# A decoder layer with a routed MoE on one core: expert weights kept for two phases, tanh in the router, wider steps in the norms

## The chip, the cores and the metric

The kernel runs on one core of one Trainium2 chip. The metric is device time in microseconds (us) of one execution. A core has TensorE (PE, with its weight loads shown apart as PEld), VectorE (DVE), ScalarE (ACT), GpSimd (POOL) and SyncE (SP), each with an instruction queue of its own that is worked off in order, and 16 DMA engines that they share.

## What is computed

A transformer decoder layer in float32 on `x` and a context, both (32, 128, 128): 32 sequences of 128 tokens with 128 features. 16 heads of 8 features, 8 experts with 512 hidden features, two experts per token.

```python
def _attn(q_in, k_in, v_in, wq, bq, wk, bk, wv, bv, wo, bo, causal):
    ...
    scores = jnp.einsum('bqhd,bkhd->bhqk', Q, Kp) / jnp.sqrt(jnp.float32(HD))
    if causal:
        mask = jnp.tril(jnp.ones((Sq, Sk), bool))
        scores = jnp.where(mask, scores, -jnp.inf)
    a = jax.nn.softmax(scores, axis=-1)
    o = jnp.einsum('bhqk,bkhd->bqhd', a, V).reshape(Bq, Sq, Dm)
    return o @ wo + bo

def _moe(x, rw, rb, w1, b1, w2, b2):
    ...
    router_weights = jax.nn.softmax(xf @ rw + rb, axis=-1)
    topw, topi = jax.lax.top_k(router_weights, K)
    topw = jax.nn.softmax(topw, axis=-1)
    combine = jnp.zeros((T, E), xf.dtype).at[jnp.arange(T)[:, None], topi].add(topw)
    h = jax.nn.gelu(jnp.einsum('td,edf->etf', xf, w1) + b1[:, None, :], approximate=False)
    eo = jnp.einsum('etf,efd->etd', h, w2) + b2[:, None, :]
    out = jnp.einsum('etd,te->td', eo, combine)
    return out.reshape(x.shape)

x = _layernorm(x + _attn(x, x, x, ..., True), ln1_g, ln1_b)
x = _layernorm(x + _attn(x, encoder_output, encoder_output, ..., False), ln2_g, ln2_b)
x = _layernorm(x + _moe(x, router_w, router_b, e_w1, e_b1, e_w2, e_b2), ln3_g, ln3_b)
```

## The kernel before, in words

**Attention.** Sequences go in groups of four. A unit is one sequence of self- (`s`) or cross-attention (`c`); 64 units run in a hand-written order, two half slots each. A half slot makes PE score one unit twice: `sc`, from which DVE takes the row maxima (L465), and two units later `st`, transposed and with the maxima subtracted, which ACT exponentiates (L473) and, for causal units, POOL masks (L477). Values, outputs and the splitting of the maxima (POOL, L491 to L494) follow in later half slots.

**Chores.** All else of a group (turning and projecting inputs, layer norm, routing, placing tokens, the biases) is written as generators. Each `yield` ends a step; `chain` and `book` put each step into a half slot by hand-written costs (`NORM`, `ROUTE`, `PLACE`: one tuple of PE, DVE, ACT and POOL times for a step) inside a window of half slots. The order of instructions on every queue is the order in which the program issues them; nothing is moved afterwards.

**Layer norm** (`normalize`): DVE statistics (L330) | DVE aggregates (L333), POOL adds epsilon and raises to −0.5 (L334, L335) | DVE makes the shift (L337) | ACT scales and shifts two sequences (L340) | ACT the other two. A bar is a `yield`. It runs 16 times in attention and 8 times on the outputs (`finish`).

**Routing** (`route`): PE logits, DVE adds the bias and subtracts the maximum (L617 to L620) | ACT exponential (L622) | DVE softmax and the eight largest (L625 to L631) | DVE their places (L634) and the difference of the two largest | ACT tanh (L640), which makes the softmax of two. `place` then counts each token's row in a table ordered by expert.

**Blocks.** Tokens' rows are scattered by POOL into a buffer in HBM (`xs`, L762, 64 scatters, one per half slot at the earliest), in two phases of four groups. Each phase has 39 blocks of 128 rows: blocks 0 to 7 belong to experts 0 to 7 and are called fixed; the expert of the other 31 is read from a table in memory (L830). A block fetches its expert's weights on SP (`wd`, 514 KB, L827 fixed or L831 dynamic), four blocks ahead into five buffers. Four blocks share a fetch of rows (`xt`, L814) and a turn: four transposes on PE (L843), four small DVE steps and the copy to `xT` (L858). A block is first layer (`ph`, PE, L866), Gelu with bias (ACT, four instructions, L871), second layer (`po`, PE, L882, one block later), copy to `ot` (DVE, L887, four buffers) and scatter to `eo` (POOL, L889).

**Beside the blocks.** `run` calls `beside` after each block. While half slots are left (the end of attention, the last routings, the row scatters of the second phase) it runs one per block; then it steps up to two `combine` generators. `combine` fetches the base (`x2d`, L955) and gathers a group's results (`gt`, L957), adds them with their weights (DVE, L974), and `finish` normalizes and applies gain and bias (L983, L985) and writes (L987).

**The start of the blocks**: at half slot `start − 6` the first four weights are fetched (`prepare`), at `start − 1` the first rows (`first_rows`), and `run` begins with the first turn.

Of the kernel before, what the change touches and what calls it, by code (L numbers as in the profile page):

```python
# [17 lines left out]
P = 128  # L18
# [44 lines left out]
def kernel(  # L63
# [260 lines left out]
    def normalize(y, name):  # L324
# [11 lines left out]
        yield  # L336
        nc.vector.scalar_tensor_tensor(rs[:, 1], mv[:, :, 0], -1.0, rs[:, 0], ALU.mult, ALU.mult)  # L337
        yield
        for t in range(G):
            nc.scalar.activation(  # L340
                y[:, t, :], y[:, t, :], AF.Identity,
                bias=rs[:, 1, t : t + 1], scale=rs[:, 0, t : t + 1],
            )
            if t == 1:
                yield
# [240 lines left out]
    def biases(gr):  # L586
# [8 lines left out]
        yield  # L595
        pw = mm_tile([G * E, P], f"pw_{gi}")
        nc.tensor.transpose(pw, w[:, 0].rearrange("p b e -> p (b e)"), ident)
        wT = small.tile([G * E, P], F32, tag="wT", name=f"wT_{gi}", bufs=2)
        nc.scalar.copy(wT, pw)
# [8 lines left out]
    def route(gr):  # L608
# [12 lines left out]
        yield  # L621
        nc.scalar.activation(lg, lg, AF.Exp)  # L622
        yield
        ls = small.tile([P, G], F32, tag="ls", name=f"ls_{gi}")
        nc.vector.tensor_reduce(ls, lg, AX.X, ALU.add)  # L625
        nc.vector.reciprocal(ls, ls)
        nc.vector.tensor_tensor(lg, lg, bc(ls, 2, E), ALU.mult)
# [4 lines left out]
        yield  # L632
        for b in range(G):
            nc.vector.max_index(idx[:, b, :], top[:, b, :], lg[:, b, :])  # L634


        ex = small.tile([P, G], F32, tag="ex", name=f"ex_{gi}")
        nc.vector.tensor_tensor(ex, top[:, :, 0], top[:, :, 1], ALU.subtract)
        yield
        nc.scalar.activation(ex, ex, AF.Tanh, scale=0.5)  # L640
# [11 lines left out]
        nc.vector.tensor_scalar(wts[:, 0, bs], ex, 0.5, 0.5, ALU.mult, ALU.add)  # L652
        nc.vector.tensor_scalar(wts[:, 1, bs], ex, -0.5, 0.5, ALU.mult, ALU.add)
# [124 lines left out]
    def pack_biases():  # L778
# [3 lines left out]
        nc.vector.tensor_copy(b1T, pb)  # L782
        nc.sync.dma_start(
# [11 lines left out]
    def weights(name):  # L795
        return moe.tile([P, 1, WP], F32, tag="wd", name=f"wd_{name}", bufs=AHEAD + 1)

    class Blocks:
# [23 lines left out]
        def fetch_weights(self, i):  # L822
            if i >= self.n:
                return
            wd = weights(f"{self.ph.p}_{i}")
            if i < NS:
                nc.sync.dma_start(out=wd[:, 0, :], in_=wpk[i])  # L827
            else:
                d = i - NS
                e = nc.sync.value_load(self.ph.tab[0:1, d : d + 1], min_val=0, max_val=E - 1)  # L830
                nc.sync.dma_start(  # L831
                    out=wd, in_=wpk[bass.ds(e, 1), :, :].rearrange("e p w -> p e w")
                )
            self.w[i] = wd[:, 0, :]
# [25 lines left out]
        def first_layer(self, i):  # L860
            w, name = self.w[i], f"{self.ph.p}_{i}"
# [8 lines left out]
            for c in range(NFC):  # L870
                nc.scalar.activation(  # L871
                    self.h[i][:, c, :], hid[:, c, :], AF.Gelu, bias=w[:, B1 + c : B1 + c + 1]
                )

        def second_layer(self, i):
# [3 lines left out]
            w, h = self.w.pop(i), self.h.pop(i)  # L879
            po = mm_tile([P, P], f"po_{p}_{i}")  # L880
            for c in range(NFC):
                nc.tensor.matmul(  # L882
                    po, lhsT=h[:, c, :], rhs=w[:, W2 + c * P : W2 + (c + 1) * P],
# [16 lines left out]
    class Pipeline:  # L900


        def __init__(self, *blocks):
            self.all = [(k, i) for k in blocks for i in range(k.n)]
            self.quads = [(k, q) for k in blocks for q in range(-(-k.n // XB))]
            self.turned = 0

        def weights(self, j):
            if j < len(self.all):
                k, i = self.all[j]  # L910
                k.fetch_weights(i)

        def prepare(self):
            for j in range(AHEAD):
                self.weights(j)
# [14 lines left out]
        def run(self, beside):  # L930

            self.turn()
            before = None
            for j, (k, i) in enumerate(self.all):
                self.weights(j + AHEAD)
# [45 lines left out]
    def finish(gr):  # L981
        yield from normalize(gr.acc, f"m{gr.gi}")
# [82 lines left out]
    NORM = (dve(1.2), (0.0, 0.9, 0.0, 1.3), dve(0.2), dve(0.0, 0.7), dve(0.0, 0.7))  # L1065
    TURN = (pe(0.45, 0.4),) * 2
    PROJECT = (pe(0.45, 0.0, 0.4),) * 2
    ROUTE = (pe(0.3, 0.0, 0.9), dve(0.0, 0.2), dve(1.2), dve(1.1), dve(0.8), dve(0.4))
# [3 lines left out]
    for gi in range(NG):  # L1072
# [36 lines left out]
        ends = chain(ends[10], ends[10] + 5, (lambda c=c: route(c), *ROUTE))  # L1109
# [149 lines left out]
```

## Time and profile before

| | |
|---|---|
| median of 9 runs | 654.76 us (650.47 to 660.95) |
| the profiled execution | 659.73 us |
| its span in the profile | 658.0 us |
| PE busy | 569.4 us, 87% of the span |
| PEld busy | 477.8 us, 73% |
| DVE busy | 409.9 us, 62% |
| ACT busy | 404.5 us, 61% |
| POOL busy | 366.9 us, 56% |
| DMA packets | 82.48 MB, mean 125 GB/s |
| attention's half slots | 0 to about 448 us, 128 of them |
| first and last block's first layer | 451.22 and 634.54 us |
| last instruction | about 658 us |

The profile follows one execution. A line of the timeline gives start, duration, engine, line of the program, operation, `out<-in` by the program's names, shapes, and how many instructions it joins; in brackets the idle time of the engine ahead of it and whose work ended that. `<-issue` is idle time in which the engine waited for nothing that the profile shows. In the list of waits a line gives engine, tile and line, what it waited for, the sum in us, how many times, and the longest. Durations are read from single instructions or means of a group; a group that joins instructions has their sum as it runs.

### The profile page before, as it was taken

To read this page: it belongs to the slowest core of one execution; us is meant where nothing else is said; L and a number is where in the kernel's file an instruction comes from. 1 tells how busy PE (TensorE), PEld (TensorE's weight loads), DVE (VectorE), ACT (ScalarE), POOL (GpSimd) and SP (SyncE) were. 2 spreads that over 40 slices of the span, in tenths; PEclk is the share of its full clock that TensorE was granted. 3 is DMA by queue.
4 is the path that set the end of the run, shared out by engine and by line. 5 is a ranking of instruction groups with operands and counts; after the bars stand their busy time and mean duration, and the time that the engine had idled before them with its cause. 6 is when DMAs were issued, how large, how long until landed. Compare 5 with 4: busy or idle time off the path is not lost. (4 is left out here: it accounts for less than half of the span.)

```text
span 658.0 us, 21902 instructions
## 1 busy us (share of the span) xinstructions
PE 569.4 (87%) x8812; PEld 477.8 (73%) x8863; DVE 409.9 (62%) x1321; ACT 404.5 (61%) x919; POOL 366.9 (56%) x747
## 2 busy tenths in 40 slices
PE   8798888899999798999999988988898878999870
PEld 6566667777777677777777767777888768998870
DVE  2455456465657866787688668885866635543463
ACT  4356576587577467766758677555675445675652
POOL 2365454344545456728836624644788885655561
PEclk9999899899999899999999989998999979999995
DMA  6110910923010011001001100331788989999972
GB/s 134 30 36 2 139 24 19 224 86 118 2 34 3 1 35 51 2 2 54 16 18 31 39 2 7 108 138 53 259 282 284 334 295 375 367 362 387 348 235 76
DMA packets 48038, 82.48 MB, mean 125 GB/s; under 512 B 7968, under 2 KB 26464, under 8 KB 47936
## 3 DMA queue, kind: packets, MB, share of 16 engines
q1 hardware_dynamic: 42816, 71.57, 34.4%
q0 software_dynamic: 4544, 9.38, 3.9%
q8 instruction: 69, 1.13, 0.7%
q14 instruction: 33, 0.27, 0.1%
q10 hardware_dynamic: 576, 0.13, 0.1%
HBM read 62.15 MB, written 23.10 MB: 130 GB/s over the span
## 5 line engine op out<-in xcount | busy, mean ns | idle before, releaser
L465 DVE TENSOR_REDUCE m_s<-sc_s 128x8 f32<-128x1024 f32 x64 | 78.3, 1224 | 79.6 <-PE st_s L450 63.8
L871 ACT ACTIVATE h<-ph,wd 128x128 f32<-128x128 f32 x312 | 88.6, 368 | 60.6 <-ACT h L871 20.6
L477 POOL TENSOR_SCALAR_AFFINE_SELECT pr_s<-pr_s 128x1024 f32<-128x1024 f32 x64 | 69.9, 1092 | 97.2 <-ACT pr_s L473 97.1
L889 POOL DMA_INDIRECT eo<-ot,to x78 | 77.5, 993 | 51.9 <-DVE acc L974 12.5
L473 ACT ACTIVATE pr_s<-st_s 128x1024 f32<-128x1024 f32 x64 | 65.7, 1026 | 61.3 <-PE st_s L450 59.4
L473 ACT ACTIVATE pr_c<-st_c 128x1024 f32<-128x1024 f32 x64 | 65.8, 1028 | 59.2 <-PE st_c L450 58.0
L465 DVE TENSOR_REDUCE m_c<-sc_c 128x8 f32<-128x1024 f32 x64 | 78.1, 1220 | 32.8 <-PE st_c L450 21.7
L866 PE MATMUL ph<-xT,wd 128*128 128x128 f32 x624 | 85.9, 282 | 9.9 <-DMA wd<-wpk 6.3
L882 PE MATMUL po<-wd,h 128*128 128x128 f32 x624 | 84.0, 278 | 6.0 <-ACT h L871 6.0
L866 PEld LDWEIGHTS ph<-xT,wd 128*128 128x128 f32 x624 | 77.5, 195 | 14.5 <-issue 3.8
L882 PEld LDWEIGHTS po<-wd,h 128*128 128x128 f32 x624 | 77.0, 194 | 6.6 <-ACT h L871 6.6
L457 PE MATMUL sc_c<-k_c,qb_c 32*128 32x128 f32 x1024 | 75.2, 285 | 4.6 <-DVE m_c L465 4.3
L457 PE MATMUL sc_s<-k_s,qb_s 32*128 32x128 f32 x1024 | 76.8, 289 | 0.3
L762 POOL DMA_INDIRECT xs<-x,slots x64 | 64.5, 1007 | 12.8 <-issue 12.2
L450 PE MATMUL st_c<-qb_c,k_c 32*128 32x128 f32 x1024 | 70.7, 274 | 0.0
L450 PEld LDWEIGHTS st_s<-qb_s,k_s 32*128 32x128 f32 x1024 | 70.2, 193 | 0.1
L450 PE MATMUL st_s<-qb_s,k_s 32*128 32x128 f32 x1024 | 70.1, 276 | 0.0
L450 PEld LDWEIGHTS st_c<-qb_c,k_c 32*128 32x128 f32 x1024 | 69.6, 189 | 0.5
L457 PEld LDWEIGHTS sc_c<-k_c,qb_c 32*128 32x128 f32 x1024 | 62.9, 188 | 6.3 <-DVE m_c L465 6.1
L457 PEld LDWEIGHTS sc_s<-k_s,qb_s 32*128 32x128 f32 x1024 | 64.3, 191 | 1.7 <-issue 1.7
L887 DVE COPY ot<-po 128x128 f32<-128x128 f32 x78 | 22.5, 289 | 61.9 <-PE po L882 52.6
L442 PEld LDWEIGHTS <-ones 32*128 32x128 bf16 x256 | 14.0, 91 | 46.3 <-issue 43.0
(243 smaller groups left out, 1196.9 us busy)
## 6 DMA issues: line engine op xcount, KB each, us to landing
wd<-wpk SPq DMA_DIRECT2D x78, 514.0 KB, 5.5
xs<-blank SPq DMA_DIRECT2D x2, 2600.0 KB
xt<-xs SPq DMA_DIRECT2D x20, 260.0 KB, 5.7
wpk<-in_L_xattn_e_w_dram SPq DMA_DIRECT2D x16, 256.0 KB, 10.8
gt<-eo SPq DMA_DIRECT2D x8, 512.0 KB, 6.7
xg<-in_x_dram SPq DMA_DIRECT2D x8, 256.0 KB, 3.9
eg<-in_ctx_dram SPq DMA_DIRECT2D x8, 256.0 KB
x2d<-base SPq DMA_DIRECT2D x8, 256.0 KB
```

The lines of the kernel that those rows point to most:

```text
L442: nc.tensor.matmul(st[:, i], lhsT=ones16[rowsof(g), :], rhs=old.mq[rowsof(g)], start=True, stop=False,)
L450: nc.tensor.matmul(st[:, i, r, :], lhsT=old.group.k[rowsof(g), old.b, :], rhs=old.group.qb[rowsof(g), old.b, r, :], start=False, stop=r == 3,)
L457: nc.tensor.matmul(sc[:, i, r, :], lhsT=new.group.qb[rowsof(g), new.b, r, :], rhs=new.group.k[rowsof(g), new.b, :], start=not new.masked, ...
L465: nc.vector.tensor_reduce(new.m[:, 8 * half : 8 * half + 8], sc.rearrange("p i r k -> p (i r) k"), AX.X, ALU.max,)
L473: nc.scalar.activation(old.pr[:, hs, :], st.rearrange("p i r k -> p (i r) k"), AF.Exp, scale=SCALE)
L477: nc.gpsimd.affine_select(out=old.pr[:, hs, :], in_=old.pr[:, hs, :], pattern=[[0, 8], [1, P]], compare_op=ALU.is_ge, fill=0.0, base=0, ch ...
L762: i = nc.gpsimd.indirect_dma_start(out=xs[ph.p][:, :], out_offset=bass.IndirectOffsetOnAxis(ap=slots[:, k, t : t + 1], axis=0), in_=gr.x2[ ...
L866: nc.tensor.matmul(hid[:, c, :], lhsT=w[:, c * P : (c + 1) * P], rhs=self.xT[i // XB][:, i % XB, :], start=True, stop=True,)
L871: nc.scalar.activation(self.h[i][:, c, :], hid[:, c, :], AF.Gelu, bias=w[:, B1 + c : B1 + c + 1])
L882: nc.tensor.matmul(po, lhsT=h[:, c, :], rhs=w[:, W2 + c * P : W2 + (c + 1) * P], start=c == 0, stop=c == NFC - 1,)
L887: nc.vector.tensor_copy(ot, po)
L889: s = nc.gpsimd.indirect_dma_start(out=eo[p][:, :], out_offset=bass.IndirectOffsetOnAxis(ap=self.to[q][:, i % XB : i % XB + 1], axis=0), i ...
```

## The change

**Weights.** The eight fixed experts' weights are fetched once, when phase 0 needs them, as two DMAs of 256 KB each (`w1`, `w2`), into buffers of attention that are done by then (`kvT`, `xT0`, `k`, and the two `pr`), and phase 1 uses them again. Their biases come from a tile that is already on chip. Dynamic blocks fetch as before, but by a count of dynamic blocks ahead, and one step later in SP's order. The first rows are fetched at `start − 5`, the first turn runs at `start − 2`; weights follow at `start − 6` (experts 0 to 2), `start − 1` (3 to 6) and `start + 1` (7).

**Routing.** Instead of exp(a) of the logits less their maximum it computes (1 + t) / (1 − t) with t = tanh(a / 2); the eight largest are taken before that, their places beside it.

**Norms, routing, biases.** Two `yield`s (three in `finish`) stand between POOL's power and DVE's L337, none between ACT's four instructions; routing and biases get further `yield`s, and the costs and windows of the booking follow.

```diff
-    def normalize(y, name):
+    def normalize(y, name, wait=2):
...
         nc.gpsimd.tensor_tensor(rs[:, 0], rs[:, 0], mhalf, ALU.pow)
-        yield
+        for _ in range(wait):
+            yield
         nc.vector.scalar_tensor_tensor(rs[:, 1], mv[:, :, 0], -1.0, rs[:, 0], ALU.mult, ALU.mult)
...
             )
-            if t == 1:
-                yield
...
         yield
+        yield
         pw = mm_tile([G * E, P], f"pw_{gi}")
         nc.tensor.transpose(pw, w[:, 0].rearrange("p b e -> p (b e)"), ident)
         wT = small.tile([G * E, P], F32, tag="wT", name=f"wT_{gi}", bufs=2)
+        yield
         nc.scalar.copy(wT, pw)
...
         nc.vector.tensor_tensor(lg, lg, bc(lm, 2, E), ALU.subtract)
-        yield
-        nc.scalar.activation(lg, lg, AF.Exp)
-        yield
+        top = small.tile([P, G, E], F32, tag="top", name=f"top_{gi}")
+        idx = small.tile([P, G, E], U32, tag="idx", name=f"idx_{gi}")
+        for b in range(G):
+            nc.vector.max(top[:, b, :], lg[:, b, :])
+        yield
+        ex = small.tile([P, G, E], F32, tag="exr", name=f"ex_{gi}", bufs=2)
+        nc.scalar.activation(ex, top, AF.Tanh, scale=0.5)
+        for b in range(G):
+            nc.vector.max_index(idx[:, b, :], top[:, b, :], lg[:, b, :])
+        yield
+        nc.vector.tensor_scalar(lg, ex, -1.0, 1.0, ALU.mult, ALU.add)
+        nc.vector.reciprocal(lg, lg)
+        nc.vector.scalar_tensor_tensor(lg, ex, 1.0, lg, ALU.add, ALU.mult)
         ls = small.tile([P, G], F32, tag="ls", name=f"ls_{gi}")
         nc.vector.tensor_reduce(ls, lg, AX.X, ALU.add)
         nc.vector.reciprocal(ls, ls)
         nc.vector.tensor_tensor(lg, lg, bc(ls, 2, E), ALU.mult)
-        top = small.tile([P, G, E], F32, tag="top", name=f"top_{gi}")
-        idx = small.tile([P, G, E], U32, tag="idx", name=f"idx_{gi}")
-        for b in range(G):
-            nc.vector.max(top[:, b, :], lg[:, b, :])
-        yield
-        for b in range(G):
-            nc.vector.max_index(idx[:, b, :], top[:, b, :], lg[:, b, :])
-
-
-        ex = small.tile([P, G], F32, tag="ex", name=f"ex_{gi}")
-        nc.vector.tensor_tensor(ex, top[:, :, 0], top[:, :, 1], ALU.subtract)
-        yield
-        nc.scalar.activation(ex, ex, AF.Tanh, scale=0.5)
+        d = small.tile([P, G], F32, tag="ex", name=f"d_{gi}")
+        nc.vector.tensor_tensor(d, lg[:, :, 0], lg[:, :, 1], ALU.subtract)
+        yield
+        yield
+        nc.scalar.activation(d, d, AF.Tanh, scale=0.5)
         idf = small.tile([P, G, 2], F32, tag="idf", name=f"idf_{gi}")
...
-        nc.vector.tensor_scalar(wts[:, 0, bs], ex, 0.5, 0.5, ALU.mult, ALU.add)
-        nc.vector.tensor_scalar(wts[:, 1, bs], ex, -0.5, 0.5, ALU.mult, ALU.add)
+        nc.vector.tensor_scalar(wts[:, 0, bs], d, 0.5, 0.5, ALU.mult, ALU.add)
+        nc.vector.tensor_scalar(wts[:, 1, bs], d, -0.5, 0.5, ALU.mult, ALU.add)
...
         return moe.tile([P, 1, WP], F32, tag="wd", name=f"wd_{name}", bufs=AHEAD + 1)
+    kept = {}
+    def fixed_weights(e):
+        if e not in kept:
+            if e < len(PLACES):
+                w = [
+                    act.tile([P, FF], F32, tag=tag, name=f"w{n}_{e}", bufs=bufs[tag])
+                    for n, tag in zip((1, 2), PLACES[e])
+                ]
+            else:
+                two = (e - len(PLACES)) % 2
+                if not two:
+                    kept["pr"] = prob.tile([P, 2, 2, FF], F32, tag="pr", name=f"w_{e}")
+                w = [kept["pr"][:, two, n] for n in range(2)]
+            nc.sync.dma_start(out=w[0], in_=wpk[e, :, :W2])
+            nc.sync.dma_start(out=w[1], in_=wpk[e, :, W2:B1])
+            kept[e] = w[0], w[1], kept["b1T"][:, NFC * e : NFC * e + NFC]
+        return kept[e]
+    bufs = {"kvT": 3, "k": 4, "xT0": 3}
+    PLACES = (("kvT", "kvT"), ("kvT", "xT0"), ("xT0", "xT0"), ("k", "k"), ("k", "k"))
...
                 return
+            if i < NS:
+                self.w[i] = fixed_weights(i)
+                return
             wd = weights(f"{self.ph.p}_{i}")
-            if i < NS:
-                nc.sync.dma_start(out=wd[:, 0, :], in_=wpk[i])
-            else:
-                d = i - NS
-                e = nc.sync.value_load(self.ph.tab[0:1, d : d + 1], min_val=0, max_val=E - 1)
-                nc.sync.dma_start(
-                    out=wd, in_=wpk[bass.ds(e, 1), :, :].rearrange("e p w -> p e w")
-                )
-            self.w[i] = wd[:, 0, :]
+            d = i - NS
+            e = nc.sync.value_load(self.ph.tab[0:1, d : d + 1], min_val=0, max_val=E - 1)
+            nc.sync.dma_start(
+                out=wd, in_=wpk[bass.ds(e, 1), :, :].rearrange("e p w -> p e w")
+            )
+            self.w[i] = wd[:, 0, :W2], wd[:, 0, W2:B1], wd[:, 0, B1:]
...
-                    self.h[i][:, c, :], hid[:, c, :], AF.Gelu, bias=w[:, B1 + c : B1 + c + 1]
+                    self.h[i][:, c, :], hid[:, c, :], AF.Gelu, bias=b[:, c : c + 1]
-            w, h = self.w.pop(i), self.h.pop(i)
+            (_, w, _), h = self.w.pop(i), self.h.pop(i)
-                    po, lhsT=h[:, c, :], rhs=w[:, W2 + c * P : W2 + (c + 1) * P],
+                    po, lhsT=h[:, c, :], rhs=w[:, c * P : (c + 1) * P],
...
             self.quads = [(k, q) for k in blocks for q in range(-(-k.n // XB))]
-            self.turned = 0
+            self.turned = self.fetched = 0
         def weights(self, j):
-            if j < len(self.all):
-                k, i = self.all[j]
+            while self.fetched < len(self.all):
+                k, i = self.all[self.fetched]
+                behind = sum(n >= NS for _, n in self.all[j : self.fetched])
+                if i >= NS and behind >= AHEAD:
+                    return
                 k.fetch_weights(i)
-
-        def prepare(self):
-            for j in range(AHEAD):
-                self.weights(j)
+                self.fetched += 1
+        def prepare(self, n0, n1):
+            for k, i in self.all[n0:n1]:
+                k.fetch_weights(i)
+            self.fetched = n1
...
-            self.turn()
             before = None
             for j, (k, i) in enumerate(self.all):
-                self.weights(j + AHEAD)
+                if j > 1:
+                    self.weights(j)
                 k.first_layer(i)
...
     def finish(gr):
-        yield from normalize(gr.acc, f"m{gr.gi}")
+        yield from normalize(gr.acc, f"m{gr.gi}", 3)
         nc.vector.tensor_tensor(gr.acc, gr.acc, bc(lng[2], 1, G), ALU.mult)
...
-    NORM = (dve(1.2), (0.0, 0.9, 0.0, 1.3), dve(0.2), dve(0.0, 0.7), dve(0.0, 0.7))
+    NORM = (dve(1.2), (0.0, 0.9, 0.0, 1.3), dve(0.0), dve(0.2), dve(0.0, 1.5))
     TURN = (pe(0.45, 0.4),) * 2
     PROJECT = (pe(0.45, 0.0, 0.4),) * 2
-    ROUTE = (pe(0.3, 0.0, 0.9), dve(0.0, 0.2), dve(1.2), dve(1.1), dve(0.8), dve(0.4))
+    ROUTE = (pe(0.3, 0.0, 0.9), dve(0.6), dve(0.9, 0.2), dve(1.5), dve(0.0), dve(0.8), dve(0.4))
     PLACE = (pe(0.2, 0.0, 1.0), pe(0.3, 0.0, 0.8), dve(1.6), dve(0.8), dve(0.6))
...
         )
-        ends = chain(ends[10], ends[10] + 5, (lambda c=c: route(c), *ROUTE))
+        ends = chain(ends[10], ends[10] + 6, (lambda c=c: route(c), *ROUTE))
         ph = phases[next(p for p, (g0, n) in enumerate(PHASES) if gi < g0 + n)]
         ends = chain(ends[-1], ends[-1] + 4, (lambda c=c, ph=ph: place(c, ph), *PLACE))
         h = ends[3]
-        chain(h, h + 5, (lambda c=c: biases(c), dve(0.6), pe(0.1, 0.3), pe(0.45, 0.0, 0.6), pool(0.0)))
+        chain(h, h + 8, (lambda c=c: biases(c), dve(0.6), dve(0.0), pe(0.1), pe(0.0, 0.3), pe(0.45, 0.0, 0.6), pool(0.0)))
         h = max(h, sent)
...
     start = max(behind, ready)
-    at(start - 6, blocks.prepare)
-    at(start - 1, blocks.first_rows)
+    at(start - 6, blocks.prepare, 0, 3)
+    at(start - 5, blocks.first_rows)
+    at(start - 2, blocks.turn)
+    at(start - 1, blocks.prepare, 3, NS - 1)
+    at(start + 1, blocks.prepare, NS - 1, NS)
```

More of the change, by code (lines that the diff above doesn't have):

```diff
@@ L620, in route @@
         nc.vector.tensor_tensor(lg, lg, bc(lm, 2, E), ALU.subtract)
-        yield
-        nc.scalar.activation(lg, lg, AF.Exp)
-        yield
[L624 to L627, printed above, removed]
         top = small.tile([P, G, E], F32, tag="top", name=f"top_{gi}")
@@ L632, in route @@
         yield
+        ex = small.tile([P, G, E], F32, tag="exr", name=f"ex_{gi}", bufs=2)
+        nc.scalar.activation(ex, top, AF.Tanh, scale=0.5)
         for b in range(G):
             nc.vector.max_index(idx[:, b, :], top[:, b, :], lg[:, b, :])
-        ex = small.tile([P, G], F32, tag="ex", name=f"ex_{gi}")
-        nc.vector.tensor_tensor(ex, top[:, :, 0], top[:, :, 1], ALU.subtract)
         yield
-        nc.scalar.activation(ex, ex, AF.Tanh, scale=0.5)
+        nc.vector.tensor_scalar(lg, ex, -1.0, 1.0, ALU.mult, ALU.add)
+        nc.vector.reciprocal(lg, lg)
+        nc.vector.scalar_tensor_tensor(lg, ex, 1.0, lg, ALU.add, ALU.mult)
+        ls = small.tile([P, G], F32, tag="ls", name=f"ls_{gi}")
+        nc.vector.tensor_reduce(ls, lg, AX.X, ALU.add)
+        nc.vector.reciprocal(ls, ls)
+        nc.vector.tensor_tensor(lg, lg, bc(ls, 2, E), ALU.mult)
+        d = small.tile([P, G], F32, tag="ex", name=f"d_{gi}")
[3 more added lines that the diff above has]
+        nc.scalar.activation(d, d, AF.Tanh, scale=0.5)
         idf = small.tile([P, G, 2], F32, tag="idf", name=f"idf_{gi}")
@@ L782, in pack_biases @@
         nc.vector.tensor_copy(b1T, pb)
+        kept["b1T"] = b1T
         nc.sync.dma_start(
@@ L860, in first_layer @@
         def first_layer(self, i):
-            w, name = self.w[i], f"{self.ph.p}_{i}"
+            (w, _, b), name = self.w[i], f"{self.ph.p}_{i}"
             pool, tag = ((ps_sc, "sc"), (ps_st, "st"))[i % 2]
```

## The prediction

> **What bounds the kernel now.** I read the busy shares by stretches first, then the waits summed over the run, then the timeline where the stretches change. The profiled execution took 659.73 us, 658.0 of it span and 1.7 around it; the median of the nine runs, 654.76, lies 0.8% below it. I sum against the profiled one and carry the difference over to the median.
>
> In the table a row is a stretch: length, busy time of PE, its weight loads, DVE, ACT, POOL with instruction counts, granted clock, share of the DMA engines, GB/s.
>
> ```profile
> 300.00:400.00 100.00, 93.42 (x1773) 74.89 (x1777) 74.09 (x228) 70.98 (x138) 57.56 (x122) 0.98 0.08 26
> 440.00:460.00 20.00, 16.16 (x214) 13.33 (x212) 12.50 (x71) 11.67 (x27) 8.89 (x17) 0.91 0.14 45
> 480.00:500.00 20.00, 17.43 (x150) 16.15 (x150) 14.79 (x74) 13.14 (x39) 16.96 (x32) 1.00 0.88 281
> 520.00:540.00 20.00, 15.44 (x116) 15.06 (x117) 8.18 (x33) 8.41 (x29) 16.85 (x31) 0.83 0.83 290
> 580.00:600.00 20.00, 19.74 (x175) 19.39 (x174) 7.26 (x31) 13.31 (x47) 11.92 (x23) 1.00 0.99 361
> 640.00:658.00 18.00, 0.00 (x0) 0.00 (x0) 7.41 (x31) 3.29 (x8) 2.54 (x4) 0.55 0.26 77
> ```
>
> So there are four regimes. Attention (to 450) is PE's, 93 of 100, with ACT and DVE at 71 and 74. The first third of the blocks (480 to 500) is POOL's: PE has 17.4 of 20, but POOL's 16.96 is 32 instructions with an issue gap before each transfer. From 544 to 638 PE and the DMA engines are both full. The last 20 us are one dependent chain without PE.
>
> POOL's pace shows in two neighbouring transfers:
>
> ```profile
> 525.11 0.96 POOL L889 DMA_INDIRECT eo<-ot,to  x1 [0.22 <-issue]
> 526.06 0.09 POOL L760 MEMSET apart<- 1x1 f32 x1
> 526.38 0.97 POOL L762 DMA_INDIRECT xs<-x,slots  x1 [0.23 <-issue]
> ```
>
> One result scatter and one row scatter per block: 2 × (0.97 + 0.22 + 0.09) = 2.56 us; blocks 13 to 28 start 2.53 us apart (487.79 to 525.80, 15 steps), against 1.79 when PE sets the pace. Then comes the one large stall:
>
> ```profile
> 532.80 1.04 POOL L335 TENSOR_TENSOR rs_m<-rs_m,mhalf 128x4 f32<-128x4 f32 x1
> ...
> 533.87 0.16 DVE L337 SCALAR_TENSOR_TENSOR rs_m<-mv_m,rs_m 128x4 f32<-128x4 f32 x1 [5.84 <-POOL rs_m L335]
> ...
> 534.07 0.88 ACT L340 ACTIVATE acc<-acc,rs_m 128x128 f32<-128x128 f32 x2 [5.99 <-DVE rs_m L337]
> ...
> 535.25 2.08 PE L882 MATMUL po<-wd,h 128*128 128x128 f32 x8 [4.12 <-ACT h L871]
> ```
>
> The power of the first output norm stands in POOL's queue behind scatters; DVE waits at L337, ACT at L340, and the Gelu behind it, hence PE.
>
> **Norm waits, in the blocks.** Now DVE's L337 stands three steps (blocks) behind POOL's pair, and ACT's four L340 one more. Block 31 starts 8.00 us after block 30 instead of 1.79, an excess of 6.2. Not all of it comes back: result scatters need their turn on POOL. From 528 to 540 POOL has only issue gaps and 0.17 <-DVE, and a copy into ot waits until the result scatter four blocks earlier has landed (at 527.74 DVE idles 2.24 for that). Results 28, 29 and 30 are scattered at 539.28, 540.65 and 541.91 whatever PE does, so copies 32 to 34 come about 2.2 us later at the earliest, 541.5 to 544.1, against 544.26, 546.04 and 548.16 now. Gain: about 3 us, from 0 to 4: in the new order one more row scatter (0.97 + 0.21 + 0.09 = 1.27) stands behind the first result scatter than now, and POOL could keep the rest. Four L340 in a row are 1.65 us (as at 643.30) instead of twice 0.88 with a Gelu set between; ACT is busy 13.31 of 20 us at 580 to 600, so it idles 0.6 per block of 1.79: I take +0.5 over all, from 0 to 1.5.
>
> **Norm waits, in attention.** DVE idles 14.6 us before L337 for the output norms (8 times) and 3.6 + 2.4 for the attention norms. The first self-attention norm's 1.5 is not moved away by the new order, nor are others wholly; at most 4.2 of the 6.0 goes. Against that, ACT's four L340 fall into one half slot. At 71 busy of 100, ACT has 0.93 us free in a half slot of 3.2; it needs 0.77 more than before where a norm falls. Summing durations by the new order per half slot, what exceeds 3.2 us rises on ACT from 9.4 to 13.7 us and on DVE from 11.2 to 13.6. A neighbouring half slot takes up much of an excess, since scores run ahead. I take 0: from −4.2 to +2.7 (6.9 of excess less 4.2).
>
> **Tanh for exp.** Eight exponentials of 0.23 become eight tanh; no row shows tanh on 128x32, its nearest are that 0.23 and tanh on 128x4 at 0.20, so nothing changes. Three DVE operations more per routing, 0.17 to 0.20 by the rows of L620, L626 and L719: 8 × 0.55 = 4.4 us of DVE; all but two of the eight routings lie in attention and are in the excess above. In return four table loads go:
>
> ```profile
> 467.65 1.28 ACT L622 ACT_TABLE_LOAD   x1
> ...
> 469.19 1.28 ACT L871 ACT_TABLE_LOAD   x1
> ...
> 470.90 1.26 PE L882 MATMUL po<-wd,h 128*128 128x128 f32 x8 [0.93 <-ACT h L871]
> ```
>
> and a second pair at 488.31 and 489.85: 4 × 1.28 = 5.1 us of ACT. PE lost 0.93 at each pair. Both lie where POOL sets the pace (its row from 468.67 on has only issue gaps), so I count 0; without that cover, −1.9.
> The Trainium skill (ScalarE: Activation LUTs, "What ACT_TABLE_LOAD costs") adds a drain of about 1.38 us to every load. Here the load at 467.65 and the exponential at 468.94 touch, and at 469.19 the next load follows; no such drain shows. By the rule ACT would get back 10.6 instead of 5.1.
>
> **Weights kept.** Eight fetches of 514 KB go, those of blocks 39 to 46, which share the window where DMA is at 0.99. PE waits for weights there 8 times:
>
> ```profile
> PE ph L866 <- DMA wd<-wpk: 6.3, 8, 2.1
> ```
>
> The waits before 549, 575 and 598 (0.81, 0.82, 0.5) stand close to the removed ones; those at 605 and 623 (1.32, 2.12) follow a group's result gather, with five buffers as before. I take −2.0: from 0 (PE is 98.7% busy there anyway) to −4. The kept tiles lie in attention's buffers: the queue on SP waits at experts 3 and 4 for the last use of k (447.9 now), and behind it stand experts 5 to 7 and dynamic fetches, the first needed at 467: nothing. The fetches are now two of 256 KB. Rows: 514 KB lands in 5.5 us, the 256 KB of xg in 3.9; both parts are on their way together and early, so 0, at most 2.3 once.
> The skill speaks against such halves (DMA: Bandwidth & Descriptors, "Measured", batch to at least 1 MiB); by its fit of 2.0 us and bytes over 436 GB/s two halves cost 5.2 against 3.2 us.
>
> **Start of the blocks.** PE's first block waits 2.50 us for the turned rows:
>
> ```profile
> 451.22 2.08 PE L866 MATMUL ph<-xT,wd 128*128 128x128 f32 x8 [2.50 <-DVE xT L858]
> ```
>
> The turn now stands two half slots earlier on PE, DVE and SP, ahead of attention's last work instead of behind it. DVE's queue still decides (busy from 443.5 to 451.2), so its copy comes perhaps 1.3 us sooner; from −2.5 (the whole wait) to +0.7 (the 0.68 of the copy in front of the last maxima). I take −1.3.
>
> **The end.** The last norm's chain keeps its steps, but the last but one's four L340 now stand behind the last Gelu on ACT, and its DVE multiply before the last copy of results at 637.80. That copy then waits for four L340 (1.65 us) and the last gather, at 641.19, follows by as much: +2.0, from 0 to +3.
>
> **Sum.** −3 + 0.5 + 0 + 0 − 2 − 1.3 + 2 = −3.8, with bounds −11 and +8 if all fell one way. The profiled time would be 655.9, and scaled to the median 654.76 × 655.9 / 659.73 = 651.
>
> **Rivals.**
> A (0.46), the sum: 651, own range 646 to 655.
> B (0.26), waits for POOL cost more than I count: attention gains the 4.2, the stall 4 instead of 3, and the table loads' 1.9 were not covered: 7.1 more than the sum, 651 − 7.1 = 643.9. For: DVE idles 20.6 us in all before L337. Against: an idle DVE beside a busy PE is no time.
> C (0.14), slower: the four L340 in one half slot hold back the exponentials behind them, and PE's next scores. Per norm 1.65 − 0.93 = 0.72; 16 in attention, 11.5 us: 651 + 11.5 = 662.5. It decides against the change from six norms on (3.8 / 0.72 is 5.3). For: at 358.64 PE waited 0.93 for an exponential right behind two L340. Against: the exponentials idle 117 us in all for PE, so mostly ACT is ahead.
> D (0.14), the stall only moves: POOL's queue holds what it held, the weights are refetched into the same full DMA window by other blocks, and only the start's 1.3 and half of the 2.0 stay, less the end's 2.0: 654.5.
>
> **How the numbers follow.** About 1% is what a measurement of this kernel can tell: the nine runs lie from 650.5 to 661.0. Faster, below 648.2: nearly all of B and a fifth of A with some of its lower end, 0.37. Slower, above 661.3: most of C, 0.13. Within: 0.50. The range leaves out the far end of B and the upper half of C: 640 to 662.
>
> **What would show it.** Right: L337's idle before the output norms falls from 14.6 to under 4; the distance from block 30 to 31 below 3 us; no table load after 455; PE's wait for weights below 4.5 us in all; the first block before 450.5; the last gather after 642. Attention decides between A, B and C: the start of block 0 less than 447 is B, beyond 455 C. Wrong: a new wait of SP for the kept tiles that delays a block, or PE idle behind L340 in many half slots.

## The result, and the profile after

The changed kernel took 668.47 us, median of 20 runs (662.46 to 672.38); the kernel before 657.88 over 62 runs. The ratio is 1.0181, with an interval of 1.0156 to 1.0206: 1.8% slower, where the prediction had 0.6% faster. Its profiled execution took 664.78 us, 663.1 of it span, 5.1 more than the span of before. Ratios compare a kernel's faster executions; the traces of norm_att, weights and route further down are of slower ones, so of them only stretches behind the start are used.

The stretches shown before, in the profile of after (columns as there):

```profile
300.00:400.00 100.00, 90.07 (x1709) 71.42 (x1713) 74.28 (x224) 68.84 (x135) 56.99 (x122) 0.98 0.09 26
440.00:460.00 20.00, 17.11 (x228) 14.89 (x228) 12.25 (x73) 11.15 (x25) 7.62 (x15) 0.91 0.59 184
480.00:500.00 20.00, 18.45 (x149) 17.35 (x147) 13.01 (x64) 11.81 (x40) 17.02 (x30) 0.92 0.75 228
520.00:540.00 20.00, 19.25 (x156) 17.80 (x157) 11.48 (x48) 11.85 (x41) 16.64 (x32) 1.00 1.00 372
580.00:600.00 20.00, 19.80 (x176) 19.54 (x176) 9.42 (x41) 12.96 (x45) 12.78 (x23) 1.00 0.99 330
640.00:663.00 23.00, 0.78 (x7) 0.59 (x6) 11.03 (x42) 5.04 (x13) 4.73 (x7) 0.58 0.25 78
```

The first row shows time lost in attention: PE does 90.1 us of work in 100 where it did 93.4. The fourth is where an engine was freed, PE 19.25 of 20 instead of 15.44, and POOL's share there is what it was, 16.6.

The large stall is gone. In the timeline of after the output norm's multiply (DVE, L338) comes up just as POOL's power ends (535.86) and does not wait for it, the four normalizations (L341) start 1.3 us later, and PE passes from block 30 (535.06) to 31 (537.66) in 2.59 us instead of 8.00:

```profile
534.82 1.04 POOL L335 TENSOR_TENSOR rs_m<-rs_m,mhalf 128x4 f32<-128x4 f32 x1
...
535.06 1.06 PE L896 MATMUL ph<-xT,wd 128*128 128x128 f32 x8
...
535.90 0.16 DVE L338 SCALAR_TENSOR_TENSOR rs_m<-mv_m,rs_m 128x4 f32<-128x4 f32 x1
...
537.22 1.65 ACT L341 ACTIVATE acc<-acc,rs_m 128x128 f32<-128x128 f32 x4
...
537.66 1.16 PE L896 MATMUL ph<-xT,wd 128*128 128x128 f32 x8 [0.21 <-DMA wd<-wpk]
```

The list of waits of after says what came in its place:

```profile
PE ph L896 <- DVE xT L888: 13.8, 5, 3.9
...
PE ph L896 <- DMA wd<-wpk: 5.2, 9, 1.0
...
DVE rs_m L338 <- POOL rs_m L335: 3.4, 2, 1.9
```

The last of them in the list of before:

```profile
DVE rs_m L337 <- POOL rs_m L335: 14.6, 8, 5.8
```

DVE's wait for POOL fell from 14.6 to 3.4, PE's for weights from 6.3 to 5.2, but PE waits 13.8 us for turned rows where it waited 2.5. One such place in the timeline of after, block 16:

```profile
497.25 0.27 DVE L917 COPY ot<-po 128x128 f32<-128x128 f32 x1
497.44 1.34 DVE L742 SCALAR_TENSOR_TENSOR fill<-more,tot 128x8 f32<-128x8 f32 x1
497.56 1.19 POOL L582 TENSOR_TENSOR x<-x,lnb 128x512 f32<-128x512 f32 x1
...
499.49 0.35 DVE L635 RECIPROCAL lg<-lg 128x32 f32<-128x32 f32 x1
...
500.84 0.29 DVE L917 COPY ot<-po 128x128 f32<-128x128 f32 x1
...
501.58 0.68 DVE L888 COPY xT<-px 128x512 f32<-128x512 f32 x1
...
502.32 0.94 PE L896 MATMUL ph<-xT,wd 128*128 128x128 f32 x6 [3.87 <-DVE xT L888]
```

Between two copies of results (497.25 and 500.84) DVE works off a step of placing (L742 on) and routing's softmax (L634 to L643) together, and the next turn's copy stands behind both.

At the end the copy that the last gather needs comes at 642.38 and the gather at 646.31, 5.1 later than before (641.19); from block 77 to the end it takes 25.1 us instead of 23.5:

```profile
642.38 0.28 DVE L917 COPY ot<-po 128x128 f32<-128x128 f32 x1
...
646.31 0.32 SPq L993 DMA_DIRECT2D gt<-eo  x1
```

### The profile page after: what moved, and what is told of

It is laid out like the page before. It is cut to its first block, busy times and chain, and to the rows that moved or that the text cites. A ratio compares the mean times of both kernels' runs of the same rounds, so it can differ in the third digit from the quotient of the medians.

```text
span 663.1 us, 21927 instructions
## 1 busy us (share of the span) xinstructions
PE 570.1 (86%) x8812; PEld 477.1 (72%) x8863; DVE 412.8 (62%) x1345; ACT 397.7 (60%) x915; POOL 366.1 (55%) x747
## 4 chain that ended last, share of the span: by engine, by line
PE 56%; DVE 17%; ACT 12%; DMA 7%; issue 4%; POOL 3%; SPq 1%; ACTq 0%; DVEq 0%; POOLq 0%
PE ph L896 8%; PE po L912 7%; PE st_s L449 6%; DVE m_s L464 5%; PE st_c L449 4%; DMA wd<-wpk 4%; PE po_s L511 3%; PE po_c L511 3%; PE sc_c L456 3%; PE st_s L441 3%; ACT pr_c L472 3%; PE sc_s L436 3%; ACT pr_s L472 3%; DVE m_c L464 3%; PE st_c L441 2%
## 5 line engine op out<-in xcount | busy, mean ns | idle before, releaser
L476 POOL TENSOR_SCALAR_AFFINE_SELECT pr_s<-pr_s 128x1024 f32<-128x1024 f32 x64 | 69.9, 1092 | 94.2 <-ACT pr_s L472 93.7
L901 ACT ACTIVATE h<-ph,wd 128x128 f32<-128x128 f32 x248 | 70.5, 369 | 63.5 <-PE ph L896 26.7
L464 DVE TENSOR_REDUCE m_c<-sc_c 128x8 f32<-128x1024 f32 x64 | 78.2, 1222 | 38.0 <-PE st_c L449 24.9
L896 PE MATMUL ph<-xT,wd 128*128 128x128 f32 x496 | 70.1, 286 | 16.4 <-DVE xT L888 10.5
L896 PEld LDWEIGHTS ph<-xT,wd 128*128 128x128 f32 x496 | 62.8, 198 | 20.4 <-DVE xT L888 11.1
L456 PE MATMUL sc_s<-k_s,qb_s 32*128 32x128 f32 x1024 | 74.7, 284 | 0.3
L449 PEld LDWEIGHTS st_s<-qb_s,k_s 32*128 32x128 f32 x1024 | 68.2, 188 | 0.1
L449 PE MATMUL st_s<-qb_s,k_s 32*128 32x128 f32 x1024 | 68.2, 271 | 0.0
L912 PE MATMUL po<-wd,h 128*128 128x128 f32 x496 | 67.3, 280 | 0.0
L456 PEld LDWEIGHTS sc_s<-k_s,qb_s 32*128 32x128 f32 x1024 | 62.4, 186 | 1.7 <-issue 1.3
L912 PEld LDWEIGHTS po<-wd,h 128*128 128x128 f32 x496 | 62.3, 197 | 0.0
```

The lines of the kernel that those rows point to most:

```text
L449: nc.tensor.matmul(st[:, i, r, :], lhsT=old.group.k[rowsof(g), old.b, :], rhs=old.group.qb[rowsof(g), old.b, r, :], start=False, stop=r == 3,)
L456: nc.tensor.matmul(sc[:, i, r, :], lhsT=new.group.qb[rowsof(g), new.b, r, :], rhs=new.group.k[rowsof(g), new.b, :], start=not new.masked, ...
L464: nc.vector.tensor_reduce(new.m[:, 8 * half : 8 * half + 8], sc.rearrange("p i r k -> p (i r) k"), AX.X, ALU.max,)
L476: nc.gpsimd.affine_select(out=old.pr[:, hs, :], in_=old.pr[:, hs, :], pattern=[[0, 8], [1, P]], compare_op=ALU.is_ge, fill=0.0, base=0, ch ...
L896: nc.tensor.matmul(hid[:, c, :], lhsT=w[:, c * P : (c + 1) * P], rhs=self.xT[i // XB][:, i % XB, :], start=True, stop=True,)
L901: nc.scalar.activation(self.h[i][:, c, :], hid[:, c, :], AF.Gelu, bias=b[:, c : c + 1])
```

## The experiments

Each run is compared with runs of the kernel before on the same chip. That matters: before took 655 to 660 us on some chips and 684 to 686 on three others, so every ratio stands beside its own before.

**First set: one part at a time on the kernel before** (one chip, before 659.2).

norm_att makes this edit for attention's norms (`wait` 2, not `split`, with the new costs in `NORM`), norm_out for the output norms (`wait` 3, not `split`); the other norms keep `wait` 1 and `split`:

```diff
-        yield
+        for _ in range(wait):
+            yield
...
-            if t == 1:
+            if split and t == 1:
                 yield
```

> Only the norms of attention change: two yields between POOL's power and DVE's L337, four ACT normalizations in a row. Theory POOL (the blocks between 469 and 545 go at the pace of POOL's queue of scatters, attention is indifferent to where a norm's steps stand): within 1 us of before. Rival ACT (four in a row hold back the exponentials, 16 times up to 0.7 us): 5 to 11 us slower, and block 0 starts 5 us or more later. My prediction had 0 here.

Measured: 659.99, ratio 0.9993 (0.9931 to 1.0054). The rival that four normalizations in a row hold back the exponentials, which was also the prediction's slower case, falls.

> Only the output norms change: three yields between POOL's power and DVE's multiply, four ACT normalizations in a row. Theory POOL: the stall of 6 us between blocks 30 and 31 goes from the records, but result scatter 30 leaves POOL no earlier than now (541.9), so blocks from 36 on gain under 1 us, and the end costs 2: 1 to 2 us slower than before. My prediction's sum: 3 off, 2.5 on, 0.5 us faster.

Measured: 659.61, ratio 1.0060 (1.0012 to 1.0109). From block 0 to 31 the trace takes 79.4 us against 86.8 before, to block 36 94.9 against 97.7, to the end 206.9 against 206.8. Of both gains 1.3 us lie between blocks 0 and 1, far ahead of the first output norm, and are not the edit's. So 6.1 us of stall are removed and 1.5 are left at block 36; result scatter 30 leaves POOL 89.4 us after block 0 instead of 90.7, sooner by no more than those 1.3, as the theory said. The rest of the blocks and the end give the gain back.

route takes over the new `route` and its booking:

```diff
-    ROUTE = (pe(0.3, 0.0, 0.9), dve(0.0, 0.2), dve(1.2), dve(1.1), dve(0.8), dve(0.4))
+    ROUTE = (pe(0.3, 0.0, 0.9), dve(0.6), dve(0.9, 0.2), dve(1.5), dve(0.0), dve(0.8), dve(0.4))
-        ends = chain(ends[10], ends[10] + 5, (lambda c=c: route(c), *ROUTE))
+        ends = chain(ends[10], ends[10] + 6, (lambda c=c: route(c), *ROUTE))
```

> Only the routing changes: tanh instead of exp, 24 more DVE operations, one more step, the new costs of its steps. Theory DVE (its steps come to lie in the half slots of placing, ahead of the turn, and the row scatters start later on POOL): PE waits for the turned rows at blocks 8 and 16 by 3 to 4 us, result scatter 30 is 2 to 4 us later than 541.9, 3 to 5 us slower. Rival (only the operations count, four table loads of 1.28 go): within 1 us of before, no such waits.

Measured: 672.33 over four runs, ratio 1.0139 (0.9969 to 1.0309): alone, this run does not show a loss. PE waits 10.9 us in four places for turned rows, 4.6 the longest. The table loads are down from six to two, and no gain from that shows.

weights takes over `fixed_weights`, the fetches by count and the earlier start:

```diff
-    at(start - 6, blocks.prepare)
-    at(start - 1, blocks.first_rows)
+    at(start - 6, blocks.prepare, 0, 3)
+    at(start - 5, blocks.first_rows)
+    at(start - 2, blocks.turn)
...
```

> Only the weights change: fixed blocks' weights fetched once, first rows fetched and turned earlier. My prediction: 3.3 us faster (1.3 at the start, 2.0 in blocks 39 to 51). Theory POOL: the start's gain is lost again in POOL's queue, the 2.0 stays: 1 to 2 us faster. Rival (PE or DMA is full there anyway): within 0.5.

Measured: 652.05, ratio 0.9912 (0.9867 to 0.9957): 5.8 us faster by the ratio, the one part with a clear gain.

**Second set: routing taken apart** (a chip on which before took 685.8).

route_ops puts the new operations into the steps and costs of before; route_steps is the run route with the exponential in place of tanh and its three operations:

```diff
-        nc.scalar.activation(lg, lg, AF.Exp)
+        nc.scalar.activation(t, lg, AF.Tanh, scale=0.5)
         yield
+        nc.vector.tensor_scalar(lg, t, -1.0, 1.0, ALU.mult, ALU.add)
+        nc.vector.reciprocal(lg, lg)
+        nc.vector.scalar_tensor_tensor(lg, t, 1.0, lg, ALU.add, ALU.mult)
...
-        nc.scalar.activation(ex, top, AF.Tanh, scale=0.5)
+        nc.scalar.activation(ex, top, AF.Exp)
```

> The router's operations alone: tanh and three more DVE operations per routing, in the steps, costs and windows of before. Theory STEPS (the new steps and costs of routing put placing and routing work side by side on DVE between two maxima): within 2 us of before, attention from first to last exponential 417 to 424 us. Rival OPERATIONS (24 more DVE operations and tanh cost it): 6 to 12 us slower, as the kernel with all of the new routing.

> The router's new steps, costs and windows, but with the exponential and without the three more operations. Theory STEPS: 6 to 12 us slower than before, attention 426 us or more, DVE's work over 3.2 us between two maxima 9 us in sum against 6. Rival OPERATIONS: within 2 us of before.

Measured: 1.0033 (0.9970 to 1.0095) and 1.0056 (0.9976 to 1.0135). Neither shows a clear loss alone; too few runs to tell them apart.

after_old_route is the change with `route` and its booking of before, weights_ops the runs weights and route_ops in one.

> The change without its routing part: weights, norms and biases as changed, routing as before. If routing alone made the change slower: 3 to 6 us faster than before (weights 5.8 off by their own run, output norms 0 to 4 on). Rival (the parts only cost together, since any of them moves the others' places): slower than before.

> Weights as changed, and tanh with its three operations in the steps of before: no norm and no bias part. If the parts add: 5 to 8 us faster than before. If the three operations cost as such: no faster than before.

Measured: 0.9928 (0.9842 to 1.0014) and 0.9962 (0.9887 to 1.0036): without the new routing the change is not slower. That put the loss into routing, not into which part of it.

**Third set: inside the changed kernel** (another chip, before 683.6), with the kernel before again for a trace there. The run bias makes only the biases' edit; after_ops is the change with the routing of route_ops, after_exp with that of route_steps.

```diff
+        yield
         pw = mm_tile([G * E, P], f"pw_{gi}")
...
+        yield
         nc.scalar.copy(wT, pw)
...
-        chain(h, h + 5, (lambda c=c: biases(c), dve(0.6), pe(0.1, 0.3), pe(0.45, 0.0, 0.6), pool(0.0)))
+        chain(h, h + 8, (lambda c=c: biases(c), dve(0.6), dve(0.0), pe(0.1), pe(0.0, 0.3), pe(0.45, 0.0, 0.6), pool(0.0)))
```

> The kernel before once more, for a trace from the same chip as the three runs beside it: as before, 28th to 124th exponential in 312 to 315 us, blocks 0 to 39 in 105.

> The biases' part alone: a step between the sums and their transposition, another ahead of the copy, a window of 8. The waits of PE for L597 (1.06, 1.64, 2.56) go. Theory POOL: they lie beside POOL's queue of scatters, so nothing comes of them: within 1.5 us of before. Rival (any moved step in attention costs): 28th to 124th exponential 4 us longer than before, 3 to 6 us slower.

> The change with routing's old steps, costs and windows, but with tanh and its three operations. Theory STEPS (the new steps are what costs): 8 to 12 us faster than the changed kernel, so 1 to 4 us faster than before; no PE wait for the turned rows of 3 to 4 us at blocks 8 and 16. Theory OPERATIONS: 4 us or more slower than before.

> The change with routing's new steps, costs and windows, but with the exponential instead of tanh and its three operations. Theory STEPS: as slow as the changed kernel within 3 us, so 6 us or more slower than before; PE's waits for the turned rows at blocks 8 and 16 stay. Theory OPERATIONS: faster than before.

Measured: before_again 686.0, its 28th to 124th exponential (numbered from 0, here and below) in 322.0 us, blocks 0 to 39 in 123.2, so the expectation taken from the other trace does not hold on this chip. Block 31 starts 2.22 us after block 30 in it: the stall that the change removes is not there on this chip. The biases' steps alone 1.0141 (1.0089 to 1.0193): a real loss that I had not costed at all. Old steps with tanh: 1.0046 (1.0010 to 1.0082), where theory STEPS had it faster than before. New steps with the exponential: 1.0205 (1.0154 to 1.0256); there PE waits 2.51 us at block 8 and less than 1.2 at block 16, so those waits are not the whole loss. Most of the loss comes with the new steps and their costs, not with the 24 operations. Whether the operations cost something of their own is not settled: without any of the new routing the change was at 0.9928, on another chip.

**Fourth set: which property of the steps.** The bookings show what the diff hides: the new `route` has six steps (five yields), its list has seven costs. The seventh is booked into a half slot of its own, holds no instruction, and `place` is chained to it. For the first group:

```
           before                          after
route      53 54 55 56 57 58               53 54 55 56 57 58 59
place      59 60 61 62 63                  60 61 62 63 64
biases     64 65 67 68                     65 66 67 69 71 72
```

The same shift of placing by one holds for all eight groups. But a step takes the half slot of its window where the engines it needs have the least booked, so the list also decides where other chores go. With six costs eleven other parts (input turns, keys, queries, values) stand elsewhere than with seven: the input turns of self-attention's group 6 at 61 and 62 instead of 55 and 59, the queries of cross-attention's group 2 at 55 and 57 instead of 57 and 58 (groups from 0). The missing entry alone moves eight of the eleven, the new values of the other six costs the remaining three. On this chip before took 683.8. place_late makes the first edit below on the kernel before, after_six the second on the changed kernel; six_old_bias is after_six with the biases' part undone, and six_best that with the output norms' part undone too.

```diff
-        ends = chain(ends[-1], ends[-1] + 4, (lambda c=c, ph=ph: place(c, ph), *PLACE))
+        ends = chain(ends[-1] + 1, ends[-1] + 5, (lambda c=c, ph=ph: place(c, ph), *PLACE))
...
-        ends = chain(ends[10], ends[10] + 6, (lambda c=c: route(c), *ROUTE))
+        ends = chain(ends[10], ends[10] + 5, (lambda c=c: route(c), *ROUTE))
-    ROUTE = (pe(0.3, 0.0, 0.9), dve(0.6), dve(0.9, 0.2), dve(1.5), dve(0.0), dve(0.8), dve(0.4))
+    ROUTE = (pe(0.3, 0.0, 1.5), dve(1.1, 0.2), dve(1.6), dve(0.0), dve(0.8, 0.2), dve(0.4))
```

> The kernel before, with nothing changed but that placing begins one half slot later in every group. Theory SHIFT (one half slot brings placing's long DVE step beside the next group's statistics at half slots 82 and 100, one row scatter more behind the first result scatter, and placing beside the turn in the blocks): 5 to 10 us slower than before, 28th to 124th exponential 5 us or more longer, 29 row scatters after the first result scatter. Rival STEPS (what lies in routing's own steps costs): within 2 us of before.

Measured: 0.9981 (0.9949 to 1.0012). A miss for the theory: moving placing alone costs nothing on this chip, although its trace has the collision at half slot 100 (5.73 us from maximum to maximum, PE idle 2.76 behind it) and 29 row scatters after the first result scatter. Its booking moves nine other parts too, but not the same ones as the change.

> The changed kernel with six costs for the six steps of routing instead of seven, and its window one shorter: placing stands where it stood before, all instructions stay. Theory SHIFT: 6 us or more faster than the changed kernel, so within 4 us of before on either side; no PE waits of 3 to 4 us for the turned rows at blocks 8 and 16. Rival STEPS: as slow as the changed kernel, 8 us or more slower than before.

> As the run with six costs, and the biases' part undone. The biases alone cost 1.4% by their own run: if that adds, 5 us or more faster than before. If it was a matter of that kernel's neighbours, as fast as with the biases changed, within 2 us.

> Weights, attention's norms and routing with six costs; biases and output norms as before. If the end costs 2 and the rest adds: 2 us faster than the run before it in this list, 6 us or more faster than the kernel before. If the stall between blocks 30 and 31 is worth more than the end: slower than that run.

Measured: 1.0062 (1.0029 to 1.0096), 1.0009 (0.9978 to 1.0040) and 0.9968 (0.9935 to 1.0001). On one chip, undoing the biases' part is worth about 0.5% and undoing the output norms' part another 0.4%, though the intervals overlap both times; six_best is not the 6 us faster that were expected. None of the ratios is below that of the weights alone (0.9912, on another chip).

**Fifth set: the pair side by side** (before 659.9).

> The changed kernel once more, on the same chip as the one with six costs. If what slows it is the same on every chip: 1.5 to 2.1% slower than before.

> The changed kernel with six costs for the six steps of routing, beside the changed kernel. Theory SHIFT: at least 0.8% of before's time faster than the changed kernel beside it, so 0.4 to 1.0% slower than before, with PE waiting for the turned rows no more than 2 us at blocks 8 and 16. Rival STEPS: within 0.4% of the changed kernel.

Measured: 671.55, ratio 1.0209 (1.0150 to 1.0267), against 661.48, ratio 1.0037 (0.9992 to 1.0083). The list of seven costs in place of six is worth 10.1 us between the medians and 1.7% between the ratios: it is most of the loss. That is the list as a whole, the entry without work and the other values together, with all that they book elsewhere. The expected waits were only partly right: with six costs PE still waits 2.40 and 3.65 at blocks 8 and 16, against 3.75 and 4.64.

Where the 8.7 us between the two spans lie, worked out from the starts of exponentials and first layers (us):

```
                 28th-124th exp  blocks 0-20  20-39  39-77  77-end
before                315.1          54.8      50.1   78.4   23.5
after                 319.8          60.9      46.8   77.9   25.1
after_again           321.2          61.5      45.9   76.8   25.7
after_six_again       315.3          57.4      45.9   77.8   25.7
weights               312.5          53.4      50.6   78.0   23.0
norm_out              312.4          53.5      48.8   79.8   24.8
route                 320.9          61.4      44.7   80.0   23.2
```

5.9 in attention and 4.1 in blocks 0 to 20. Before runs attention's program exactly as weights and norm_out do; its 315.1 holds 2.2 more than those in one group of half slots.

The traces of the pair from 40 us to the last block's first layer (columns as in the stretches above), after_again first:

```profile
40.00:644.58 604.58, 551.68 (x8528) 457.60 (x8519) 390.24 (x1283) 378.00 (x870) 350.08 (x698) 0.97 0.37 121
40.00:635.86 595.86, 545.37 (x8579) 452.68 (x8579) 391.56 (x1283) 379.79 (x873) 351.77 (x704) 0.99 0.38 124
```

Over all PE idles 2.4 us longer in after_again, and it is busy 6.3 us longer with the same work; in attention's stretch alone 5.3 of the 5.9 are idle time. The granted clock is at half for 34.1 us of the first trace's stretch and for 10.2 of the second's, and matmuls are slower at half clock: a block's first layer takes 421 ns a matmul between 487.7 and 490.9 (clock 0.50) and 275 between 491.1 and 494.4 (1.00). PE waits for more than 2 us seven times in these two stretches; behind six of the seven a stretch of 3.4 us at half clock begins within 1.3 us. So these waits cost more than their length.

One place where a shift costs attention 3.4 us (96th to 100th exponential, 16.0 against 12.5) is in the timeline of after_again at half slots 100 and 101. Between two maxima DVE has the long step of placing (L725 to L740) and then the next group's statistics:

```profile
356.57 1.23 DVE L464 TENSOR_REDUCE m_c<-sc_c 128x8 f32<-128x1024 f32 x1 [0.78 <-PE st_s L449]
...
358.04 0.77 DVE L725 SCALAR_TENSOR_TENSOR moved<-pos,move 128x32 f32<-128x32 f32 x1
...
360.49 1.09 POOL L476 TENSOR_SCALAR_AFFINE_SELECT pr_s<-pr_s 128x1024 f32<-128x1024 f32 x1 [1.72 <-ACT pr_s L472]
360.58 1.02 DVE L740 TENSOR_TENSOR slots<-si,ri 128x8 uint32<-128x8 uint32 x1
361.52 0.86 DVE L330 BATCH_NORM_STATS2 st_c<-y_c 128x6 f32<-128x128 f32 x4
362.30 1.20 DVE L464 TENSOR_REDUCE m_c<-sc_c 128x8 f32<-128x1024 f32 x1
...
363.56 0.38 PE L456 MATMUL sc_c<-k_c,qb_c 32*128 32x128 f32 x2 [2.48 <-DVE m_c L464]
```

5.73 us from maximum to maximum, and PE, which needs the buffer that the maximum reads for its next scores, idles 2.48. In the timeline of after_six_again the same two pieces stand one maximum apart:

```profile
349.22 1.23 DVE L464 TENSOR_REDUCE m_c<-sc_c 128x8 f32<-128x1024 f32 x1 [0.41 <-PE sc_c L456]
...
350.85 0.20 DVE L725 SCALAR_TENSOR_TENSOR moved<-pos,move 128x32 f32<-128x32 f32 x1
...
352.86 0.17 DVE L740 TENSOR_TENSOR slots<-si,ri 128x8 uint32<-128x8 uint32 x1
...
353.68 1.22 DVE L464 TENSOR_REDUCE m_c<-sc_c 128x8 f32<-128x1024 f32 x1
...
354.95 0.38 PE L456 MATMUL sc_c<-k_c,qb_c 32*128 32x128 f32 x2 [0.42 <-DVE m_c L464]
...
355.76 0.86 DVE L330 BATCH_NORM_STATS2 st_c<-y_c 128x6 f32<-128x128 f32 x4
```

4.46 us, and PE idles 0.42. The wait itself is 2.06 us longer in after_again, and behind it the clock is at half from 364.7 to 368.1. From the 96th to the 100th exponential PE idles 2.15 us longer and is busy 1.27 longer than in after_six_again, where the clock stays at full.

## Why the prediction was wrong

**The step that failed** is "I take 0: from −4.2 to +2.7" for attention. It compared sums of durations per half slot and let neighbours take up the excess. Attention's stretch became 7 to 9 us longer than in the runs of the old order (319.8, 321.2 and 320.9 against 312.4 and 312.5; 315.1 in before's own trace), and with six costs it is back at 315.3. DVE's busy time over 3.2 us from the start of one maximum to the next, measured afterwards, sums to 5.4 to 5.8 us in the old order and 8.4 in the new: up by about as much as the sums had said (+2.4). But PE idles 31.9 us in that stretch of after against 24.9 in norm_out, 10.7 of it for late maxima against 8.4, and the half-clock stretches behind long waits stood in no sum. The attribution was wrong too: attention's norms, which rival C blamed, show no cost (0.9993, 0.9931 to 1.0054); the booking of routing does, and I read the seven costs without counting the steps they were for.

**Terms that were missing.** The biases' steps have no line in the sum. Alone they cost 1.4% on one chip, inside the change about 0.5% on another. And I priced routing's operations only as attention work: two routings and three placings lie in blocks 0 to 20, and those blocks take 60.9 instead of 54.8 us. Blocks 20 to 39 give part back, 46.8 instead of 50.1, and not only by the removed stall: in route, which leaves the norms alone, they take 44.7, with block 31 only 3.12 us behind block 30. POOL's queue, which set the pace there before, would explain that; it was not tested apart.

**A term of the wrong size, and a wrong sum.** The stall: 3 expected net, about 1.5 measured to block 36 by norm_out, and nothing of it at the end. The lower bound of the sum, −11, is also not what its terms give: −4, −4.2, −4 and −2.5 make −14.7, without the table loads. The upper one, +8, is right, and the medians differ by +10.6.

**Terms that held.** The end: +2.0 expected, +1.6 in the trace of after, +1.3 in that of norm_out. Start: −1.3 expected; from the 124th exponential to block 0 weights alone takes 9.7 instead of 10.9. The kept weights: −2.0, and blocks 39 to 51 take 22.8 instead of 24.3; as a whole that part gave 5.8 with an interval of 2.8 to 8.8, against 3.3 expected. The four ACT normalizations in the blocks: +0.5 expected; norm_out's blocks 39 to 77 take 1.4 more.

**Signs to watch.** L338's idle before the output norms (3.4, under 4), the distance from block 30 to 31 and the last gather came as written; the last table load stands at 451.02. Block 0 at 452.33 (forecast before 450.5) and the weights' waits of 5.2 (below 4.5) did not. Block 0 was also to tell the rivals apart: 452.33, between 447 and 455, would have meant A, so this sign misled.

**What stays open**: why moving placing alone, on the kernel before, costs nothing, while the list of seven costs is worth 1.7% in the changed kernel. The two were measured on different chips and with different routing steps beside placing. The collision at half slot 100 costs place_late time as well (96th to 100th exponential 15.5 us, 13.9 in before_again), but the clock stays at full behind its wait, and other stretches are shorter. Between the 52nd and the 56th exponential, where after_again takes 14.6 us and after_six_again 12.1, place_late takes 11.7, as the kernel before; there the queries of group 2 stand at half slots 55 and 57 in place_late, before and after_six_again, and at 57 and 58 in after_again. Whether the entry, the values or which moved neighbour decides was not tried.

## What to carry to other kernels

Where a list of costs books the work of a generator, count both: an entry too many is a delay of everything chained to it, the list also moves what is booked beside it, and the diff shows neither. A removed wait can be worth only what the slowest queue beside it leaves over, here 1.5 of 6.1 us. Where PE needs a result of DVE every 3 us, judge a moved step by which other steps it comes to lie beside, slot by slot, not by sums, and read the granted clock behind every long wait.

## What the runs showed of the hardware

A small DVE operation that meets a tensor operation of POOL can end only with it: L742 took 1.34 us at 497.44 beside POOL's L582, and 0.15 to 0.18 elsewhere; L740 took 1.02 beside POOL's L476, and 0.17 in the same place of the other kernel. It is not the rule: in after 154 operations of DVE that take under 0.3 us by their median start during a tensor operation of POOL of over 0.9 us, and 19 of them were stretched, each to its end. So a long step of many small operations can grow by a microsecond when it meets POOL.

The same kernel before differs by 4% between chips (659 and 684 us). In the blocks of a slower one more and longer pauses show (103.8 us for blocks 0 to 31 of before_again against 86.8): up to block 39 ACT has eleven of 2.1 to 6.8 us, seven of them with no releaser in the records (four over 2 us in before), and the granted clock is at half for 29.6 us, against 9.7 in before. I didn't find their cause.

Runs of one kernel lie some 7 us apart by the clock granted in the first 33 us. Here is that row of the page of after (40 slices, tenths):

```profile
PEclk9999999999999899999998999998998998999995
```

and of after_again, with 5 in its second slice:

```profile
PEclk9599899999999889999998999996988998999995
```

The first exponential comes at 23.7 us in the one and 30.7 in the other. That is part of why the profiled spans differ by 5.1 us and the medians by 10.6: after's profiled run (664.78) began at full clock and lies under its median. That of before (659.73) began so too, and lies over its own; what slowed it was not found.
